# Two of four layer norms: results written by ScalarE with a scale and a shift instead of by VectorE

## The chip, the core and the metric

The kernel runs on one NeuronCore of a Trainium2 chip. The core has a matrix engine (TensorE, "PE" in the profile, with its weight loads as "PEld"), VectorE ("DVE"), ScalarE ("ACT"), GpSimd ("POOL") and SyncE ("SP", which here only issues transfers). Each engine works through its own queue of instructions in order. Where an instruction needs another engine's result it waits for a semaphore, and everything behind it in its queue waits too.

The metric is the device time of one execution in microseconds, smaller is better. The time before is 2995.68 us, the median of 3 runs (2994.83 to 2996.52).

## The reference

Two graph layers are applied one after the other to 64 graphs of 256 nodes with 256 features, in float32. The first is a pair of graph attention steps, a layer norm, a feed-forward block with relu and a second layer norm. The second is an attention of 8 heads whose values depend on the relation between two nodes, a third layer norm, a feed-forward block with gelu and a fourth layer norm. Cut to what matters here:

```python
def _layernorm(x, g, b):
    mu = jnp.mean(x, axis=-1, keepdims=True)
    var = jnp.var(x, axis=-1, keepdims=True)
    return (x - mu) * jax.lax.rsqrt(var + EPS) * g + b

# layer 0
h = _gat(_gat(x, adj, W1, a1, F), adj, W2, a2, F)
h = _layernorm(x + h, g_ln1, b_ln1)                        # first norm, "A"
ff = relu(h @ w_ff1 + b_ff1) @ w_ff2 + b_ff2
src = _layernorm(h + ff, g_ln2, b_ln2)                     # second norm, "B"
# layer 1
attn_out = heads(src, adj) @ Wo + bo
x = _ln(src + attn_out, g1, beta1)                         # third norm, "C"
ff = gelu(x @ W1 + b1) @ W2 + b2
out = _ln(x + ff, g2, beta2)                               # fourth norm, "D"
```

## The kernel before

**Tiles.** A graph's 256 nodes lie as two halves of 128 partitions with 256 features each, so a tile of node rows is 128 x 2 x 256. Matmul results land in PSUM, in eight banks that all products share in turn (`mm_tile`). Everything else is in SBUF.

**Order.** No scheduler is at work. The computation of a graph is cut into some 150 pieces with names such as `G.nmA`, and a list written out by hand (`PERIOD`, line 45) says in which order the pieces of several graphs follow each other. `F.u1/2` means: piece `F.u1` of the graph that entered two periods ago. The lags go up to 6, so parts of seven graphs are in flight. `START` fills this pipeline and `END` drains it, each with an order of its own, and the loop between them runs 58 times. Each engine gets its instructions in this order and keeps to it. Two stretches of the list matter here, with the norm pieces among the pieces around them:

```python
T.lnC/4 T.fk3/5 A.dt10/3 A.ex02/3 T.fp3/5 T.rsC/4 F.fa/2 G.gA0/1 A.mg11/3 F.u0/2 T.nmC/4 F.u1/2 T.dtC/4 ...
... T.hk2/5 G.rsA/2 T.hp1/5 A.sp01/4 A.dm01/4 T.hc/5 A.mg10/4 T.hk3/5 G.nmA/2 F.raB/4 F.dtA/2 T.hd/5 A.vk2/4 G.most/1 T.hp3/5 G.eA/1 T.hp2/5 ... T.he/5
```

**A layer norm** (`layernorm`, line 562) has three pieces. `ln` (`sums`, line 569) adds the residual and takes mean and variance on VectorE (lines 576 and 577), and ScalarE adds the small constant to the variance (line 579). `rs` (`root`, line 581) raises that to the power -1/2 on GpSimd (line 583). `nm` (`norm`, line 596) writes the result `y`: without `scalar`, by two VectorE instructions of 128 x 256 that subtract the mean and multiply by the root (line 601). With `scalar=True`, `root` has two more GpSimd instructions on 128 x 2 elements that form the shift, minus mean times root, in place of the mean (lines 586 and 587), and `norm` writes `y` by two ScalarE activations with that shift as bias and the root as scale (`norm_to`, line 591). Before the change, norm B passes `scalar=True`; norm D writes its result into PSUM in the same way (`weighted`). For A and C the input of the norm lies in PSUM (`gat_b` and `wo` in the profile), for B and D in SBUF.

**What follows a norm.** `dt` turns 32 x 32 squares of `y` on VectorE (line 542, `sq_a`, `sq_c`), `dm` and `mg` store them to device memory and load them back rearranged (lines 546 and 553, issued by SP), so that features lie on partitions (`cols_a`, `cols_c`). `ra` and `rb` multiply `y` by the gain and add the shift of the norm on GpSimd (lines 629 and 634), for the next residual.

**Products.** The two products of a feed-forward block and the projections are done by seven products of quarter size instead of eight (`seven_products`, line 692). Their pieces are `ha` to `he` for the first product and `fa` to `fe` for the second, in PSUM banks X, Y and Z. Banks X and Y keep on accumulating while results are taken out in between: `hk1`, `hk2`, `hk3`, `hk4` are copies out of a bank by ScalarE (line 770, tile `hid_c` or `hid_a`), `hp1`, `hp2`, `hp3` are adds by VectorE (line 734). So `T.he` may begin only once `T.hp2` has read bank X (`hX_c`). The second product needs sums of quarters of the hidden tile, made by GpSimd in `F.u0` to `F.u3` (line 676, tile `H_a`): `F.fb` needs `u0`, `F.fc` needs `u1` and then `u3`, `F.fd` needs `u2`.

Of the kernel before, what the change touches and what calls it, by code (L numbers as in the profile page):

```python
# [210 lines left out]
def binary(ctx: ExitStack, tc: tile.TileContext, t, most, out: bass.AP):  # L211

    nc = tc.nc
    x, xT, adjT = t["x"], t["xT"], t["adjT"]
# [18 lines left out]
    def mm_tile(name, shape=(P, 2, 256)):  # L233
        return psum.tile(list(shape), F32, tag="mm", name=name, bufs=8)
# [195 lines left out]
    graphs, tiles, warmed = {0: {}}, {}, []  # L430
# [98 lines left out]
    def over_nodes(name):  # L529
        return rows[name].unsqueeze(1).to_broadcast([P, NT, D])  # L530
# [31 lines left out]
    def layernorm(do, stage, key, name, src, last=None, scalar=False):  # L562

        tiles = {}

        def sums():
            acc, *residual = src()
            if residual:  # L570
                nc.vector.tensor_tensor(acc, acc, *residual, ALU.add)
            tiles["acc"] = acc
            stats = small.tile([P, NT, 6], F32, tag="stats", name=f"stats_{name}", bufs=2)
            mv = tiles["mv"] = small.tile([P, NT, 2], F32, tag="mv", name=f"mv_{name}")
            for i in range(NT):
                nc.vector.bn_stats(stats[:, i, :], acc[:, i, :])
                nc.vector.bn_aggr(mv[:, i, :], stats[:, i, :])
            tiles["var"] = small.tile([P, NT], F32, tag="var", name=f"var_{name}")
            nc.scalar.activation(tiles["var"], mv[:, :, 1], AF.Identity, bias=eps)

        def root():
            tiles["rstd"] = small.tile([P, NT], F32, tag="rstd", name=f"rstd_{name}")
            nc.gpsimd.tensor_tensor(tiles["rstd"], tiles["var"], neghalf, ALU.pow)
            if scalar:
                tiles["shift"] = tiles["mv"][:, :, 0]
                nc.gpsimd.tensor_tensor(tiles["shift"], tiles["shift"], tiles["rstd"], ALU.mult)
                nc.gpsimd.tensor_scalar(tiles["shift"], tiles["shift"], -1.0, 1.0, ALU.mult, ALU.mult)

        def norm_to(y):
            for i in range(NT):  # L590
                nc.scalar.activation(
                    y[:, i, :], tiles["acc"][:, i, :], AF.Identity,
                    bias=tiles["shift"][:, i : i + 1], scale=tiles["rstd"][:, i : i + 1],
                )

        def norm():
            y = tiles["y"] = work.tile([P, NT, D], F32, tag="y", name=f"y_{name}", bufs=3)
            if scalar:
                return norm_to(y)
            for i in range(NT):  # L600
                nc.vector.tensor_scalar(
                    y[:, i, :], tiles["acc"][:, i, :],
                    tiles["mv"][:, i, 0:1], tiles["rstd"][:, i : i + 1], ALU.subtract, ALU.mult,
                )

        def weighted():

            tiles["n"] = mm_tile(f"n_{name}")
            norm_to(tiles["n"])

        def finished():
            tiles["res"] = work.tile([P, NT, D], F32, tag="res", name=f"res_{name}", bufs=3)
            nc.vector.tensor_tensor(tiles["n"], tiles["n"], over_nodes(last[0]), ALU.mult)
            nc.vector.tensor_tensor(tiles["res"], tiles["n"], over_nodes(last[1]), ALU.add)

        do[f"{stage}.ln{key}"], do[f"{stage}.rs{key}"] = sums, root
        if last:
            do[f"{stage}.nm{key}"], do[f"{stage}.rb{key}"] = weighted, finished
        else:
            do[f"{stage}.nm{key}"] = norm  # L620
        return tiles

    def scaled(do, stage, key, name, tiles, g, b):


        def times():
            tiles["res"] = work.tile([P, NT, D], F32, tag="res", name=f"res_{name}", bufs=3)
            for i in range(NT):
                nc.gpsimd.tensor_tensor(
                    tiles["res"][:, i, :], tiles["y"][:, i, :], rows[g], ALU.mult  # L630
                )

        def plus():
            nc.gpsimd.tensor_tensor(tiles["res"], tiles["res"], over_nodes(b), ALU.add)

        do[f"{stage}.ra{key}"], do[f"{stage}.rb{key}"] = times, plus

    def to_columns(do, stage, key, name, tiles, pairs=False):

        def out():
            sq = work.tile([P, 4, NT * KC * 32], F32, tag="sq", name=f"sq_{name}", bufs=2)
            flat = sq.rearrange("p b n -> p (b n)")
            if pairs:
                return flat, sq.rearrange("p b (t r k) -> p t k b r", t=NT, k=KC)
            return flat, flat

        def rows():
            y = tiles["y"]  # L650
            if pairs:
                return y.rearrange("p t (k b c) -> p t k b c", k=KC, b=4)
            return y.rearrange("p t (k b c) -> p b (t k) c", k=KC, b=4)

        def into():
            cols = work.tile([P, KC * N], F32, tag="cols", name=f"cols_{name}", bufs=3)
            if pairs:
                tiles["cols"] = cols.rearrange("p (n k) -> p k n", k=KC)
            else:
                tiles["cols"] = cols.rearrange("p (a t k r) -> p k t a r", a=4, t=NT, k=KC)  # L660
            return cols.rearrange("p (a n) -> p a n", a=4)

        turned(do, stage, key, f"y_{name}", P, rows, into, out)
# [14 lines left out]
    def combine(do, stage, key, name, tiles):  # L678


        def sums():
            s = tiles["S"] = work.tile([P, 4, P], F32, tag="S", name=f"S_{name}", bufs=3)
            cols = tiles["cols"]
            blocks = [block(cols, c, i) for i in range(NT) for c in range(KC)]
            sums = [s[:, n, :] for n in range(4)]
            if len(blocks[0].shape) == 3:
                sums = [n.rearrange("p (a r) -> p a r", a=4) for n in sums]
            add_sums(nc.gpsimd, blocks, sums, range(4))

        do[f"{stage}.s{key}"] = sums  # L690
# [133 lines left out]
    def gat(do, b, tiles):  # L824


        t = {}
# [123 lines left out]
            do[f"G.ad{step}"], do[f"G.ex{step}"] = partial(maximum, step), partial(exps, step)  # L951
            do[f"G.rz{step}"] = partial(over_sums, step, width)
        do["G.gB"] = second
        return layernorm(do, "G", "A", f"a{b}", lambda: (t["gat"], tiles["x"]))

    def projections(do, b, tiles):

# [168 lines left out]
    def graph(b, do, tiles):  # L1126
        a = gat(do, b, tiles)
        to_columns(do, "F", "A", f"a{b}", a)
        scaled(do, "F", "A", f"a{b}", a, "L0_gnn_g_ln1", "L0_gnn_b_ln1")
        combine(do, "F", "A", f"a{b}", a)  # L1130
        feed_forward(do, "F", f"a{b}", a, lambda: ff0, "r", AF.Relu)
        y = layernorm(do, "F", "B", f"b{b}", lambda: (a["ff"],), scalar=True)
        to_columns(do, "F", "B", f"y{b}", y, pairs=True)
        scaled(do, "F", "B", f"b{b}", y, "L0_gnn_g_ln2", "L0_gnn_b_ln2")
        combine(do, "F", "B", f"y{b}", y)
        heads = attention(do, b, projections(do, b, y), tiles)
        c = layernorm(do, "T", "C", f"c{b}", lambda: (heads["wo"], y["res"]))
        to_columns(do, "T", "C", f"c{b}", c)
        scaled(do, "T", "C", f"c{b}", c, "L1_gnn_g1", "L1_gnn_beta1")
        combine(do, "T", "C", f"c{b}", c)  # L1140
        feed_forward(do, "T", f"c{b}", c, ff1, "ge", AF.Gelu, b >= B - LAST)
        d = layernorm(
            do, "T", "D", f"d{b}", lambda: (c["ff"],), ("L1_gnn_g2", "L1_gnn_beta2"), True
        )

        def store():
            nc.sync.dma_start(out=out[b].rearrange("(t p) d -> p t d", p=P), in_=d["res"])

        do["T.out"] = store


    E = mybir.EngineType
    graph(0, graphs[0], tiles[0])
    order = [(piece, int(lag)) for piece, lag in (entry.split("/") for entry in PERIOD)]
    lags = max(lag for _, lag in order)

    def run(piece, b):
        if piece.startswith("S."):
            return setup.pop(piece)()
        if piece.startswith("W."):  # L1160
            return warm(4, wx[:, 0, :D])
        if b not in graphs:
            graphs[b] = {}
            graph(b, graphs[b], load(graphs[b], b))
        graphs[b].pop(piece)()

    with tc.manual_schedule(engines={E.PE, E.DVE, E.Activation, E.Pool, E.SP}):
        for entry in START:
            piece, b = entry.split(":")
# [4 lines left out]
        for entry in END:  # L1174
            piece, b = entry.split(":")
# [306 lines left out]
```

## Time and profile before

| | |
|---|---|
| median of 3 runs | 2995.68 us |
| the profiled execution | 2995.85 us |
| its span, from the first to the last instruction | 2994.0 us |
| ScalarE: `y_b` (line 591), mean of one | 593 ns, 128 times |
| VectorE: `y_a` and `y_c` (line 601), mean of one | 540 and 531 ns, 128 times each |
| GpSimd: `rstd_a`, `rstd_c` (line 583), mean of one | 702 and 701 ns, 64 times each |
| GpSimd: `mv_b` lines 586 and 587, mean of one | 197 and 193 ns, 64 times each |
| GpSimd: `mv_d` lines 586 and 587, mean of one | 208 and 490 ns, 64 times each |
| mean granted TensorE clock | 0.995 of full speed |

The span is a little shorter than the execution's time, because that also holds what lies before the first and after the last instruction of the program. Busy times count an engine's own work and not its waiting. Instructions of one engine overlap at their ends, so the distance between two starts can be shorter than the duration shown. A row such as `y_a<-gat_b,mv_a,rstd_a` names the tile written and the tiles read. In a timeline, `x2` are two like instructions shown as one row, and a bracket tells how long the engine sat idle before the row and whose instruction ended that.

### The profile page before, as it was taken

The page shows a single profiled execution, that of the slowest core. Times are in us where ns is not written, and L with a number is a line of the kernel's source. Part 1 is how long each engine was busy: PE and PEld are TensorE (multiplying, and loading weights), DVE is VectorE, ACT ScalarE, POOL GpSimd, SP SyncE. Part 2 cuts the span into 40 slices and gives each one's busy share as a digit, 9 for nine tenths or more (in the row PEclk, how much of TensorE's full clock was granted, in tenths as well). Part 3 has the DMA queues.
Part 4 walks back from the last instruction along what each step waited for, and adds up shares of the span by engine and source line. Part 5 has one row for each costly group of instructions (what it writes and reads, how often), then busy time and mean ns, then how long its engine had stood idle before and what let it go on. Part 6 is the DMA issues. An engine that isn't in the chain of part 4 may idle for free.

```text
span 2994.0 us, 75422 instructions
## 1 busy us (share of the span) xinstructions
PE 2947.4 (98%) x25662; PEld 2673.7 (89%) x25662; DVE 2603.0 (87%) x6250; ACT 2234.8 (75%) x6401; POOL 2287.4 (76%) x3455
## 2 busy tenths in 40 slices
PE   8999999999999999999999999999999999999997
PEld 7889999999999999999899999999899998999986
DVE  4888889888889888898898898888898898898885
ACT  3677787787777777777777777777777877877764
POOL 6777778777777777778778778777777787777785
PEclk9999999999999999999999999999999999999999
DMA  5544444444444444444454444454444444444442
GB/s 138 157 149 158 151 148 157 153 148 159 149 150 156 147 152 153 151 153 154 151 155 152 153 156 149 152 159 146 149 160 149 152 157 152 146 159 151 132 156 86
DMA packets 401891, 449.27 MB, mean 150 GB/s; under 512 B 41152, under 2 KB 342720, under 8 KB 401504
## 3 DMA queue, kind: packets, MB, share of 16 engines
q1 hardware_dynamic: 399984, 442.14, 46.3%
q8 instruction: 209, 3.42, 0.5%
q0 software_dynamic: 976, 1.72, 0.3%
q14 instruction: 178, 1.46, 0.2%
q10 hardware_dynamic: 544, 0.52, 0.1%
HBM read 242.90 MB, written 201.33 MB: 148 GB/s over the span
## 4 chain that ended last, share of the span: by engine, by line
PE 91%; POOL 3%; DVE 2%; DMA 2%; issue 1%; ACT 1%; SPq 0%; POOLq 0%; DVEq 0%; ACTq 0%
PE hX_a L758 8%; PE o L1082 8%; PE fX_a L796 7%; PE hX_c L758 7%; PE fX_c L796 7%; PE sc L1024 4%; PE wo L1103 4%; PE qX L967 4%; PE hY_a L758 4%; PE hY_c L758 4%; PE fY_c L796 4%; PE fY_a L796 4%; PE gat_a L930 3%; PE wh L847 3%; PE gat_b L930 3%; PE vX L991 3%
## 5 line engine op out<-in xcount | busy, mean ns | idle before, releaser
L1071 DVE SCALAR_TENSOR_TENSOR pm<-away,pm 128x512 f32<-128x512 uint8 x512 | 359.2, 712 | 4.6 <-DMA pm<-far_p 4.2
L542 DVE STREAM_TRANSPOSE p<-p 128x1024 f32<-128x1024 f32 x256 | 315.4, 1232 | 4.2 <-POOL p L1057 4.1
L1082 PE MATMUL o<-pm,v 128*32 128x256 f32 x4096 | 235.4, 381 | 0.1
L776 ACT ACTIVATE hid_c<-hid_c,col_L_gnn_b 128x256 f32<-128x256 f32 x512 | 231.5, 505 | 1.7 <-DVE hid_c L734 0.4
L776 ACT ACTIVATE hid_a<-hid_a,col_L_gnn_b_ff 128x256 f32<-128x256 f32 x512 | 224.4, 501 | 2.2 <-DVE hid_a L734 2.0
L796 PE MATMUL fX_a<-f_L_gnn_w_ff,hid_a 128*128 128x128 f32 x1536 | 203.8, 276 | 1.7 <-DVE acc_a L734 1.3
L796 PEld LDWEIGHTS fX_a<-f_L_gnn_w_ff,hid_a 128*128 128x128 f32 x1536 | 196.0, 192 | 10.5 <-DVE acc_a L734 2.3
L796 PE MATMUL fX_c<-f_L_gnn_W,hid_c 128*128 128x128 f32 x1536 | 203.5, 275 | 0.8 <-DVE acc_c L734 0.4
L1082 PEld LDWEIGHTS o<-pm,v 128*32 128x32 f32 x4096 | 126.5, 110 | 85.5 <-issue 0.9
L796 PEld LDWEIGHTS fX_c<-f_L_gnn_W,hid_c 128*128 128x128 f32 x1536 | 191.8, 192 | 5.6 <-DVE acc_c L734 0.6
L770 ACT COPY hid_a<-hX_a 128x512 f32<-128x512 f32 x192 | 113.2, 590 | 60.5 <-PE hX_a L758 60.1
L676 POOL TENSOR_TENSOR S_y<-cols_y 128x128 f32<-128x128 f32 x128 | 65.5, 512 | 118.7 <-DMA cols_y<-far_y_y 118.4
L1024 PE MATMUL sc<-kT,qT 32*128 32x256 f32 x2048 | 146.6, 400 | 2.5 <-DVE kT L988 2.4
L758 PE MATMUL hX_a<-S_a,f_L_gnn_w_ff 128*128 128x128 f32 x1024 | 144.1, 284 | 0.0
L864 ACT COPY wh_B<-gat_a 128x258 f32<-128x258 f32 x124 | 46.4, 375 | 129.7 <-PE gat_a L930 129.7
L758 PEld LDWEIGHTS hX_c<-cols_c,f_L_gnn_W 128*128 128x128 f32 x1024 | 131.1, 191 | 13.0 <-DVE hid_c L734 3.1
L758 PEld LDWEIGHTS hX_a<-S_a,f_L_gnn_w_ff 128*128 128x128 f32 x1024 | 124.0, 191 | 19.6 <-issue 19.2
L758 PE MATMUL hY_c<-S_c,f_L_gnn_W 128*128 128x128 f32 x1024 | 139.5, 279 | 0.0
L796 PE MATMUL fY_a<-f_L_gnn_w_ff,H_a 128*128 128x128 f32 x1024 | 137.8, 277 | 0.7 <-DVE acc_a L809 0.6
L758 PE MATMUL hX_c<-cols_c,f_L_gnn_W 128*128 128x128 f32 x1024 | 135.3, 275 | 2.8 <-DVE hid_c L734 2.5
L796 PE MATMUL fY_c<-f_L_gnn_W,H_c 128*128 128x128 f32 x1024 | 136.4, 276 | 1.5 <-POOL H_c L676 0.9
L758 PE MATMUL hX_a<-cols_a,f_L_gnn_w_ff 128*128 128x128 f32 x1024 | 135.9, 276 | 0.0
(2845 smaller groups left out, 10573.6 us busy)
## 6 DMA issues: line engine op xcount, KB each, us to landing
far_p<-p SPq DMA_DIRECT2D x256, 512.0 KB, 3.0
pm<-far_p SPq DMA_DIRECT2D x1024, 128.0 KB, 2.9
adj<-in_adjT SPq DMA_DIRECT2D x64, 256.0 KB, 3.3
far_y_a<-sq_a SPq DMA_DIRECT2D x64, 256.0 KB, 2.1
cols_a<-far_y_a SPq DMA_DIRECT2D x256, 64.0 KB, 2.0
far_y_y<-sq_y SPq DMA_DIRECT2D x64, 256.0 KB, 2.0
cols_y<-far_y_y SPq DMA_DIRECT2D x256, 64.0 KB, 2.0
far_y_c<-sq_c SPq DMA_DIRECT2D x64, 256.0 KB, 2.0
```

What stands on the lines that cost most here:

```text
L542: nc.vector.transpose(to, rows)
L758: nc.tensor.matmul(ps[:, f * P : (f + 1) * P], weights()[0][:, factor, f * P : (f + 1) * P], left, start=start and f == 0, stop=f == FC // ...
L770: nc.scalar.copy(hidden(i, h), ps.rearrange("p (f n) -> p f n", n=P))
L776: nc.scalar.activation(tiles["hid"][:, f, :], tiles["hid"][:, f, :], func, bias=b1[:, f : f + 1])
L796: nc.tensor.matmul(ps, left[:, f, :], weights()[2][:, factor, f * P : (f + 1) * P], start=start and f == 0, stop=f == FC // 2 - 1, skip_gr ...
L847: nc.tensor.matmul(t["whp", j], tiles["xT"][:, c, nodes(j)], wx[:, c, :], start=(c == 0), stop=(c == KC - 1),)
L930: nc.tensor.matmul(ps, t["s"][:, j, nodes(i)], t["whz"][:, j, :width], start=(j == 0), stop=(j == NT - 1),)
L967: nc.tensor.matmul(ps[:, nodes(n)], w[:, factor, :], right, start=start and n == 0, stop=n == 1, skip_group_check=True,)
L1024: nc.tensor.matmul(t["sc", g, hh][:, i, :], qkv["q"][hd, g, nodes(i)], qkv["k"][hd, g, :], start=True, stop=True,)
L1071: nc.vector.scalar_tensor_tensor(pm[:, 1], tiles["away"].rearrange("p (a n) -> p a n", a=4), 0.0, pm[:, 0], ALU.is_equal, ALU.mult,)
L1082: nc.tensor.matmul(ps[hh * DH : (hh + 1) * DH, :], qkv["v"][:, j, d0 : d0 + DH], t["pm", (g, hh)][:, r].rearrange("p a (j t r) -> p j t a ...
L1103: nc.tensor.matmul(t["wo"][:, i, :], t["oT"][:, c, nodes(i)], late["wo"][:, c, :], start=(c == 0), stop=(c == KC - 1),)
```

## The change

Norms A and C now pass `scalar=True` as norm B does. Nothing else is touched: `PERIOD`, `START` and `END` stay as they are, and the pieces `G.rsA`, `G.nmA`, `T.rsC` and `T.nmC` keep their places in them.

```diff
-        return layernorm(do, "G", "A", f"a{b}", lambda: (t["gat"], tiles["x"]))
+        return layernorm(do, "G", "A", f"a{b}", lambda: (t["gat"], tiles["x"]), scalar=True)
...
-        c = layernorm(do, "T", "C", f"c{b}", lambda: (heads["wo"], y["res"]))
+        c = layernorm(do, "T", "C", f"c{b}", lambda: (heads["wo"], y["res"]), scalar=True)
```

For each graph VectorE loses four instructions (two of line 601 for each norm), ScalarE gains four of line 591, and GpSimd gains two of line 586 and two of line 587. On ScalarE the new instructions of A stand between the copy of `T.hk3` (`hid_c<-hX_c`) and `G.most` (`adj`, line 839), and those of C between the exponentials of `A.ex02` and `A.ex03`. On GpSimd they stand right behind `rstd_a` and `rstd_c`; behind those of C come `F.u0`, `F.u1`, `F.u3` and `F.u2`. TensorE's and SP's instructions and their order are the same.

## The prediction

> **What bounds the kernel now.** I read first the busy times of the page and the chain of waits:
>
> ```profile
> PE 2947.4 (98%) x25662; PEld 2673.7 (89%) x25662; DVE 2603.0 (87%) x6250; ACT 2234.8 (75%) x6401; POOL 2287.4 (76%) x3455
> ...
> PE 91%; POOL 3%; DVE 2%; DMA 2%; issue 1%; ACT 1%; SPq 0%; POOLq 0%; DVEq 0%; ACTq 0%
> ```
>
> TensorE is busy in all but 46.6 us of the span (2994.0 - 2947.4), and 91% of the chain is its own work. So unloading VectorE saves almost nothing; what counts is whether anything that TensorE waits for comes later. In the longest pieces of the chain the wo product (L1103) starts at 1893.41 and again at 1938.54: a period is 45.13 us. The written order runs 58 such periods (lag 6 of 64 graphs), each with one first norm (A) and one third norm (C).
>
> So I read one period, engine by engine, in the timeline (start, duration, engine, line; in brackets idle time and who ended it). First norm, VectorE, ScalarE and the weight loads:
>
> ```profile
> 1596.74 0.99 DVE L601 TENSOR_SCALAR y_a<-gat_b,mv_a,rstd_a 128x256 f32<-128x256 f32 x2
> 1597.77 0.71 DVE L542 STREAM_TRANSPOSE sq_a<-y_a 128x512 f32<-128x512 f32 x1
> 1598.41 0.38 DVE L1006 TENSOR_TENSOR v<-vY,row_bv 128x256 f32<-128x256 f32 x1
> 1598.71 0.67 DVE L734 TENSOR_TENSOR hid_c<-hid_c,hY_c 128x512 f32<-128x512 f32 x1
> 1599.48 0.69 DVE L734 TENSOR_TENSOR hid_c<-hid_c,hX_c 128x512 f32<-128x512 f32 x1
> ```
> ```profile
> 1597.58 0.59 ACT L770 COPY hid_c<-hX_c 128x512 f32<-128x512 f32 x1 [0.31 <-PE hX_c L758]
> 1598.06 0.73 ACT L839 ACTIVATE adj<-adj,minus_one 128x512 int32<-128x512 int32 x1
> ```
> ```profile
> 1586.22 0.97 PEld L796 LDWEIGHTS fY_a<-f_L_gnn_w_ff,H_a 128*128 128x128 f32 x8
> ...
> 1600.22 0.89 PEld L758 LDWEIGHTS hX_c<-cols_c,f_L_gnn_W 128*128 128x128 f32 x7
> ```
>
> The last product into hX_c (T.he) starts loading weights at 1600.22, and the add that must first read hX_c out of its bank (T.hp2) ends at 1599.48 + 0.69 = 1600.17. That is 0.05 us, and it is 51 to 53 ns for the same two instructions in 60 of the 64 graphs: **this add has no slack at all** before TensorE. It stands fourth on VectorE behind y_a.
>
> Third norm, GpSimd:
>
> ```profile
> 1581.53 0.70 POOL L583 TENSOR_TENSOR rstd_c<-var_c,neghalf 128x2 f32<-128x2 f32 x1 [1.12 <-ACT var_c L579]
> 1582.19 1.28 POOL L676 TENSOR_TENSOR H_a<-hid_a 128x512 f32<-128x512 f32 x1
> 1583.55 1.27 POOL L676 TENSOR_TENSOR H_a<-H_a,hid_a 128x512 f32<-128x512 f32 x1
> 1584.90 1.27 POOL L676 TENSOR_TENSOR H_a<-hid_a,H_a 128x512 f32<-128x512 f32 x1
> ```
>
> The third H_a (F.u3) ends at 1586.17 and the weight load of fY_a that takes it starts at 1586.22, again 0.05 us, in 61 graphs of 64. Three adds queue right behind rstd_c, which itself waited for var_c, so for TensorE's wo product through VectorE: the chain hangs on TensorE and can't start earlier.
>
> **What the change costs, part by part.** Removed: two TENSOR_SCALAR on VectorE for each norm, 0.99 us a pair for A, 0.98 for C (L601). Added for each norm: two small GpSimd operations (L586, L587) behind rstd, and a pair of ScalarE activations (L591). The second norm shows the prices:
>
> ```profile
> 1592.73 0.84 POOL L583 TENSOR_TENSOR rstd_b<-var_b,neghalf 128x2 f32<-128x2 f32 x1 [0.88 <-ACT var_b L579]
> 1593.65 0.20 POOL L586 TENSOR_TENSOR mv_b<-mv_b,rstd_b 128x2 f32<-128x2 f32 x1
> 1593.94 0.19 POOL L587 TENSOR_SCALAR mv_b<-mv_b 128x2 f32<-128x2 f32 x1
> ```
>
> *GpSimd.* From the end of rstd_b (1593.57) to the end of L587 (1594.13): 0.56 us. The fourth norm's row gives the upper end: rstd_d ends at 1611.61, its L587 at 1612.50, 0.89 us, because L587 took 0.52 there while VectorE ran a masking multiply (pm, L1071). Beside the new operations of A and C VectorE stands waiting for y, so I take 0.56.
>
> The Trainium skill ("SBUF — State Buffer", "Who interferes with whom") says that a VectorE operation with two SBUF inputs shuts GpSimd out of a port that they share until it ends. The 0.52 beside pm agrees; by the rule the price is 0.56 where no such operation runs, and 0.89 where one does, some 19 us more over 58 periods.
>
> *ScalarE.* The nearest row is y_b, 1.09 us the pair, but from SBUF; y_a and y_c are read from PSUM. Pairs with a bias column take 0.91 from SBUF (hid_a, L776) and 0.84 from PSUM (s_B, L884), so I take 1.09 - 0.08 = 1.01. Ends: 0.84 (that s_B, without a scale column) and 1.20 (n_d, written to PSUM).
>
> *First norm, on the path.* The activations stand behind the copy of hX_c, which waits for TensorE, so they start at 1598.06, where adj starts now; mv_a is ready by 1596.71 + 0.56 = 1597.27. y_a is done at 1599.07 instead of 1597.73. VectorE has nothing it may do meanwhile: its queue is in order, and sq_a is next. Then sq_a at 1599.10, v at 1599.74 (+0.64, as now), the two hid_c adds at 1600.04 (+0.30) and 1600.64 (+0.60, the usual step of such an add), the last ending at 1601.33: 1.16 us later than 1600.17. The weight loader idles 0.10 before 1600.22 now, so I count half of that off: **1.11 us a period** (0.89 to 1.35 with the ends of the pair, and all or none of the 0.10). What else comes late finds TensorE late too: the gelus of hid_c behind y_a wait for the same add; ScalarE's qT and kT copies move about 1.2 us, and so do the products around them. On SP the store of sq_a moves from 1598.51 to about 1599.85 and holds up the loads of cols_y behind it. cols_y lands at 1602.32 and is used from 1603.45 on: both move by about the same, and the 1.1 us between them remain. Were that cover gone, it would cost up to 0.2 us a period.
>
> *Third norm, on the path.* H_a comes 0.56 later at each of its steps. The first had 0.6 us of slack (weight load at 1584.07, add over at 1583.47), the second 0.46, the third none: **0.56 us a period** (0.46 to 0.89). ScalarE waits 0.5 us for mv_c with the exponentials queued behind it, and y_c is done at 1582.83 + 1.01 = 1583.84, 0.32 later than now. I cost both at nothing: ScalarE idles 1.21 us before its next copy (wh_B at 1584.48) and reaches it some 0.2 late, just before e_B; VectorE idles 0.54 before 1585.37. Without these covers they would run beside the 0.56 and not on top of it.
>
> *Fill and drain.* In the first 173 and last 149 us TensorE is busy 155.9 and 121.9 us. Six norms of each kind lie there. If all hit TensorE as above they cost 6 x 1.67 = 10 us; if VectorE's queue ends each wait they save 12 x 0.98 = 12. I take nothing.
>
> Sum: 58 x (1.11 + 0.56) = 97 us. The profiled execution took 2995.85 us (span 2994.0), 0.17 above the median of the runs, so 2995.7 + 97 = **3092 us**.
>
> Two sentences of the Trainium skill pull against each other here. "ScalarE: Activation LUTs" ("Rules for kernel authors") wants additions and products on VectorE, and "Perfetto Trace Analysis" ("Optimizing Scalar/DVE Operations") lets work go from VectorE to ScalarE once VectorE is saturated. VectorE's 87% would invite the second, at best for the 46.6 us that TensorE idles, 2949 us; the two gaps of 0.05 us say that neither decides, since queue places set the price.
>
> **Rivals.** (1) *Only one of the two stalls lands*, the other meeting slack that one period doesn't show: 58 x 1.11 gives 3060, 58 x 0.56 gives 3028. Against: the 0.05 us repeats in 60 and in 61 graphs. (2) *More queues suffer*: ScalarE carries 2.0 us more work a period, and products of q and k (0.5 us between ScalarE's copy ending at 1604.74 and the product at 1605.24) or the landing of cols_y stall too. With 0.5 us a period more, 29 us: 3121. For: the order leaves little air. Against: all of these sit behind the stall and move with TensorE. (3) *Faster*: VectorE's queue gets its 0.99 us back ahead of T.hp2, because y_a is written before sq_a's turn. It decides if y_a ends on ScalarE before 1597.73; then TensorE loses only part of its 46.6 us of idling, say 30: 2966. Against: y_a would have to start at 1596.7, ahead of a copy that stands before it and waits for TensorE until 1597.58. (4) *The operations don't move*: the built order of both kernels shows y_a on ScalarE right behind the hX_c copy and y_c between two pairs of exponentials, so this gets 1%, at 2996.
>
> **Chances.** Forecast 0.68, rival 1 0.12, rival 2 0.14, rival 3 0.03, no change 0.03 (rival 4, or everything hidden). A measurement tells some 0.2%, 6 us, from no change. Corner sums are 58 x (0.89 + 0.46) - 12 = 66 and 58 x (1.35 + 0.89) + 10 = 140 us; with part of rivals 1 and 2 the range is 3058 to 3130. Faster 0.03, same 0.03, slower 0.94.
>
> **What would show it.** A period of about 46.8 us; VectorE idle some 1.4 us before sq_a, released by ScalarE's y_a; TensorE idle before T.he about 1.1 us, released by VectorE's hid_c, and about 0.5 before fY_a, released by GpSimd's H_a; both new waits in every period. Wrong if the period stays below 45.6 us, if the idle time of TensorE sits at other products, or if y_a starts on ScalarE before 1598.06 of this period's time.

## The result, and the profile after

The changed kernel takes 3098.07 us (median of 4 runs, 3096.15 to 3098.76), the kernel before beside it 2996.10 us (2994.83 to 2997.69). The ratio is **1.0342, with a 95% interval of 1.0329 to 1.0354: 3.4% slower**. The prediction was 3092 us, range 3058 to 3130.

The busy times of the page of the changed kernel:

```profile
PE 3003.0 (97%) x25662; PEld 2674.9 (86%) x25662; DVE 2473.2 (80%) x5994; ACT 2348.3 (76%) x6657; POOL 2341.9 (76%) x3711
```

VectorE is 130 us less busy than before (2603.0) and ScalarE 114 us more (2234.8), so the change did what it says. TensorE has the same 25662 products and 56 us more of modelled busy time, which is a warning: its ends are modelled, and the weight loads, whose busy time stays at 2674.9 us (2673.7 before), don't show it, so I take it for waiting that is counted as work. The weight loads show the waits better. What the weight loads and VectorE waited for, in total, how often, and the longest, in the changed kernel:

```profile
PEld hX_c L758 <- DVE hid_c L734: 54.8, 60, 1.9
PEld vY L991 <- DVE v L1006: 29.4, 58, 0.5
...
PEld fY_a L796 <- POOL H_a L676: 23.3, 61, 0.7
```
```profile
DVE sq_a L542 <- ACT y_a L591: 152.2, 63, 3.1
DVE sq_c L542 <- ACT y_c L591: 78.1, 62, 1.9
```

In the kernel before, the weight loads of hX_c waited for hid_c 3.1 us in all, three times, and those of fY_a for H_a 0.6 us, twice. Here they come about once a period. VectorE's new idle time (230 us) is far more than the total loss: most of it costs nothing, and only what delays TensorE counts.

One period, first norm, in the timeline of the changed kernel: ScalarE, VectorE, weight loads.

```profile
1604.55 0.59 ACT L770 COPY hid_c<-hX_c 128x512 f32<-128x512 f32 x1 [0.31 <-PE hX_c L758]
1605.03 1.03 ACT L591 ACTIVATE y_a<-gat_b,mv_a,rstd_a 128x256 f32<-128x256 f32 x2
```
```profile
1602.98 0.65 DVE L734 TENSOR_TENSOR hid_c<-hid_c,hZ_c 128x512 f32<-128x512 f32 x1
1606.09 0.71 DVE L542 STREAM_TRANSPOSE sq_a<-y_a 128x512 f32<-128x512 f32 x1 [2.46 <-ACT y_a L591]
1606.72 0.39 DVE L1006 TENSOR_TENSOR v<-vY,row_bv 128x256 f32<-128x256 f32 x1
1607.03 0.67 DVE L734 TENSOR_TENSOR hid_c<-hid_c,hY_c 128x512 f32<-128x512 f32 x1
1607.63 0.67 DVE L734 TENSOR_TENSOR hid_c<-hid_c,hX_c 128x512 f32<-128x512 f32 x1
```
```profile
1607.16 0.30 PEld L991 LDWEIGHTS vY<-f_Wv,S_y 128*128 128x128 f32 x2 [0.51 <-DVE v L1006]
1608.35 0.97 PEld L758 LDWEIGHTS hX_c<-cols_c,f_L_gnn_W 128*128 128x128 f32 x8 [0.89 <-DVE hid_c L734]
```

y_a starts 0.48 us after the start of the copy, where adj stood before, and VectorE stands idle for 2.46 us with sq_a at the head of its queue. The last add of hX_c ends at 1608.30 and the weight load follows at 1608.35, the same 0.05 us as before. The weight loads show two pauses, 0.51 and 0.89 us; the first is an earlier station of the same delay.

Third norm, GpSimd and the weight load that takes its third sum:

```profile
1587.94 0.70 POOL L583 TENSOR_TENSOR rstd_c<-var_c,neghalf 128x2 f32<-128x2 f32 x1 [1.33 <-ACT var_c L579]
1588.72 0.20 POOL L586 TENSOR_TENSOR mv_c<-mv_c,rstd_c 128x2 f32<-128x2 f32 x1
1589.01 0.19 POOL L587 TENSOR_SCALAR mv_c<-mv_c 128x2 f32<-128x2 f32 x1
1589.17 1.27 POOL L676 TENSOR_TENSOR H_a<-hid_a 128x512 f32<-128x512 f32 x1
1590.51 1.28 POOL L676 TENSOR_TENSOR H_a<-H_a,hid_a 128x512 f32<-128x512 f32 x1
1591.87 1.27 POOL L676 TENSOR_TENSOR H_a<-hid_a,H_a 128x512 f32<-128x512 f32 x1
```
```profile
1593.19 0.97 PEld L796 LDWEIGHTS fY_a<-f_L_gnn_w_ff,H_a 128*128 128x128 f32 x8 [0.38 <-POOL H_a L676]
```

The small operations end 0.56 us after rstd_c (1589.20 - 1588.64). The three sums follow, and the last ends 0.05 us before the weight load again.

**Where the 103 us of the profiled executions went** (spans 3097.0 and 2994.0). I compared the distances between the starts of neighbouring weight loads in the two traces, step by step in the periodic part. Only a few steps grew:

| Step | a period, median |
|---|---|
| the loads for vY and the last product into hX_c, 0.482 - 0.107 + 0.797 - 0.036 | +1.14 us |
| the loads that take the second and the third sum H_a, 0.141 + 0.413 | +0.55 us |
| the period, from one wo product to the next | 45.13 to 46.82, +1.69 us |

On average over the periods it is 1.63 us and not 1.69: in the kernel before, the loads of cols_y land late now and then, and 0.09 us a period of that now hides behind the new wait. From the second wo product to the sixtieth, 58 periods, the time grew from 2624.8 to 2719.1 us, by 94.3. The part before that grew by 2.8 us and the part after it by 5.9.

### The profile page after: what moved, and what is told of

Same layout as the page of the kernel before. It is cut to its first block, busy times and chain, and to the rows that moved or that the text cites. A ratio compares the mean times of both kernels' runs of the same rounds, so it can differ in the third digit from the quotient of the medians.

```text
span 3097.0 us, 75750 instructions
## 1 busy us (share of the span) xinstructions
PE 3003.0 (97%) x25662; PEld 2674.9 (86%) x25662; DVE 2473.2 (80%) x5994; ACT 2348.3 (76%) x6657; POOL 2341.9 (76%) x3711
## 5 line engine op out<-in xcount | busy, mean ns | idle before, releaser
L1071 DVE SCALAR_TENSOR_TENSOR pm<-away,pm 128x512 f32<-128x512 uint8 x512 | 348.9, 693 | 5.0 <-DMA pm<-far_p 4.6
L676 POOL TENSOR_TENSOR S_y<-cols_y 128x128 f32<-128x128 f32 x128 | 76.3, 596 | 139.2 <-DMA cols_y<-far_y_y 139.2
L542 DVE STREAM_TRANSPOSE sq_a<-y_a 128x512 f32<-128x512 f32 x64 | 45.6, 712 | 152.2 <-ACT y_a L591 152.2
L796 PEld LDWEIGHTS fY_a<-f_L_gnn_w_ff,H_a 128*128 128x128 f32 x1024 | 128.6, 191 | 27.7 <-POOL H_a L676 23.3
```

The lines of the kernel that those rows point to most:

```text
L542: nc.vector.transpose(to, rows)
L676: engine.tensor_tensor(to[i], one, other, op)
L796: nc.tensor.matmul(ps, left[:, f, :], weights()[2][:, factor, f * P : (f + 1) * P], start=start and f == 0, stop=f == FC // 2 - 1, skip_gr ...
L1071: nc.vector.scalar_tensor_tensor(pm[:, 1], tiles["away"].rearrange("p (a n) -> p a n", a=4), 0.0, pm[:, 0], ALU.is_equal, ALU.mult,)
```

## The experiments

Each run is compared with the kernel before on the same chip; the period is the median distance of the wo products. The medians of the kernel before lie between 2992.22 and 2996.10 us on the chips used, so a difference between two absolute times is good to some 4 us.

| Run | median, us | ratio to before, 95% interval | period, us |
|---|---|---|---|
| the change | 3098.07 | 1.0342 (1.0329 to 1.0354) | 46.82 |
| first norm alone | 3055.51 | 1.0201 (1.0184 to 1.0218) | 46.26 |
| third norm alone | 3030.20 | 1.0113 (1.0096 to 1.0130) | 45.68 |
| small GpSimd steps alone | 3025.66 | 1.0098 (1.0081 to 1.0115) | 45.68 |
| first sum ahead of the root | 3149.25 | 1.0508 (1.0490 to 1.0525) | 47.75 |
| turning later | 3074.15 | 1.0272 (1.0255 to 1.0289) | 46.31 |
| turning later, loads first | 3065.96 | 1.0245 (1.0228 to 1.0262) | 46.21 |
| y_a ahead of the copy | 3069.00 | 1.0254 (1.0237 to 1.0271) | 46.24 |
| all three moves | 3118.55 | 1.0418 (1.0401 to 1.0436) | 47.17 |
| shifts on VectorE | 3099.86 | 1.0351 (1.0334 to 1.0368) | 46.87 |
| third norm, shift on VectorE | 3037.21 | 1.0140 (1.0124 to 1.0157) | 45.74 |
| shifts on VectorE, y_a ahead | 3063.48 | 1.0231 (1.0214 to 1.0248) | 46.18 |
| third norm, shift on ScalarE | 3000.63 | 1.0024 (1.0014 to 1.0033) | 45.13 |

### One norm at a time

```diff
-        c = layernorm(do, "T", "C", f"c{b}", lambda: (heads["wo"], y["res"]), scalar=True)
+        c = layernorm(do, "T", "C", f"c{b}", lambda: (heads["wo"], y["res"]))
```

> Only the first norm is written by ScalarE; the third stays on VectorE. Theory (two separate stalls, each set by a place in a queue, which add): TensorE waits some 1.14 us a period before the last product into hX_c, and no longer before fY_a; 58 periods give 66 us, and about half of the 9 us of fill and drain comes on top: 3065 to 3070 us. Rival (the loss is the extra work of ScalarE, which is the same for both norms): half of the 102 us, 3047 us.

It took 3055.51 us. The wait is the one of the full change to the last digit, and there is none before fY_a:

```profile
PEld hX_c L758 <- DVE hid_c L734: 54.8, 60, 1.9
PEld vY L991 <- DVE v L1006: 29.4, 58, 0.5
```

The period grew by 1.13 us, 1.14 expected. The total is 10 us below my figure, because the periods grew by 60.2 us and not 66 (the landings of cols_y that now hide), and fill and drain lost nothing.

The other way round, with the first norm's call put back and the third's left as changed:

> Only the third norm is written by ScalarE; the first stays on VectorE. Theory: 0.55 us a period before fY_a, released by GpSimd's H_a, nothing before the last product into hX_c; 32 us and some 4 us of fill and drain: 3030 to 3035 us. Rival (extra work of ScalarE): 3047 us. Rival (the third norm's stall is there only because the first norm's stall has moved TensorE): 2996 to 3002 us.

3030.20 us, as the first theory had it. The weight loads of this run have one new wait:

```profile
PEld fY_a L796 <- POOL H_a L676: 23.2, 61, 0.7
```

The same amount, as often, as in the full change (23.3 us, 61 times): the stall doesn't need the first norm's. Period growths of 1.13 and 0.55 add up to the 1.69 of both, within 0.01. An even share of ScalarE's extra work (3047 us for either run) is refuted.

### The third norm: which of its parts costs the time

The kernel before, with the two operations added and nothing moved:

```diff
+            if stage == "T" and not scalar:
+                spare = tiles["var"]
+                nc.gpsimd.tensor_tensor(spare, tiles["mv"][:, :, 0], tiles["rstd"], ALU.mult)
+                nc.gpsimd.tensor_scalar(spare, spare, -1.0, 1.0, ALU.mult, ALU.mult)
```

> The kernel before, with the two small GpSimd operations of the shift added behind rstd_c for the third norm, into a tile that nothing reads; VectorE still writes y_c. Theory (the third norm's loss is the GpSimd queue alone): as with the third norm on ScalarE, 0.55 us a period before fY_a, 3028 to 3033 us. Rival (the loss comes from VectorE and ScalarE waiting for y_c): no change, 2996 us.

3025.66 us, and a period of 45.68 us, the same as with the third norm on ScalarE:

```profile
PEld fY_a L800 <- POOL H_a L680: 23.4, 61, 0.7
```

Two operations on 256 numbers each, whose result nobody reads, cost 30 us, because three sums that TensorE waits for stand behind them.

Then I tried to take them out of the way by order:

```diff
-A.ex02/3 T.fp3/5 T.rsC/4 F.fa/2 G.gA0/1 A.mg11/3 F.u0/2 T.nmC/4 F.u1/2 T.dtC/4 F.fk1/2 A.rz02/3
+A.ex02/3 T.fp3/5 F.u0/2 T.rsC/4 F.fa/2 G.gA0/1 A.mg11/3 T.nmC/4 F.u1/2 T.dtC/4 F.fk1/2 A.rz02/3
```

> Both norms on ScalarE; in the periodic order alone, the first sum for the feed-forward block (F.u0) stands before the third norm's root on GpSimd. Theory: the first sum then runs while GpSimd waits for the variance, the three sums end about 0.6 us earlier, and the wait before fY_a goes: a period of 46.3 us, 3098 - 32 = 3066 us. Rival (the wait is not of this queue): 3098 us.

The theory's number was wrong by 83 us: 3149.25, slower than the change itself. GpSimd in one period of this run, the weight load, and what the products behind it waited for in the whole run:

```profile
1566.12 1.27 POOL L676 TENSOR_TENSOR H_a<-hid_a 128x512 f32<-128x512 f32 x1 [1.68 <-PE fY_c L796]
1567.35 0.70 POOL L583 TENSOR_TENSOR rstd_c<-var_c,neghalf 128x2 f32<-128x2 f32 x1
```
```profile
1569.78 0.97 PEld L796 LDWEIGHTS fY_a<-f_L_gnn_w_ff,H_a 128*128 128x128 f32 x8 [1.49 <-issue]
```
```profile
PE fY_a L796 <- ACT y_c L591: 64.2, 58, 1.4
```

I had overlooked two dependencies. The first sum can't start early: `H_a` and `H_c` share one buffer (`bufs=1`), so it waits for the product fY_c to have read the old one, and now the root waits behind it. And fY_a's bank in PSUM is the one that y_c is read from (the wo bank, handed on when y_c is done). With the root late, y_c was late, and TensorE lost 1.35 us before fY_a; the profile names ScalarE's y_c for 58 waits of the product fY_a, 64.2 us. What this run does show is that a later y_c is a second price of the third norm. In this run y_c ends 0.11 us ahead of the first weight load of fY_a (median); in the full change it ends 0.23 us ahead, 0.55 in the kernel before, and the step before that load is 0.22 us in both, so there the second price isn't paid.

### The first norm: places in the queues

Both norms on ScalarE, the turning of y_a two adds later in VectorE's queue:

```diff
-T.hk3/5 G.nmA/2 F.raB/4 F.dtA/2 T.hd/5 A.vk2/4 G.most/1 T.hp3/5 G.eA/1 T.hp2/5 T.ge0/5 F.dmB/3
+T.hk3/5 G.nmA/2 F.raB/4 T.hd/5 A.vk2/4 G.most/1 T.hp3/5 F.dtA/2 G.eA/1 T.hp2/5 T.ge0/5 F.dmB/3
```

> Both norms on ScalarE; in the periodic order alone, the turning of y_a on VectorE (F.dtA) stands two adds later, just ahead of T.hp2. Theory (the first norm's loss is VectorE standing idle at the turning with the adds of hX_c behind it): the two pieces before it fill the wait, T.hp2 ends some 0.36 us later than in the kernel before in place of 1.16, so 0.7 to 0.8 us a period come back, less up to 0.15 where the loads of cols_y wait on SP behind the store of sq_a: 3050 to 3064 us. Rival (ScalarE's added work delays what follows on ScalarE): 3098 us.

3074.15 us: 24 us come back (21 by the ratios), less than the 34 to 48 expected. The wait before the last product into hX_c fell from 1.14 to 0.34 us a period, as worked out. But TensorE now waits elsewhere (products of this run):

```profile
PE qX L967 <- DMA cols_y<-far_y_y: 11.6, 15, 1.8
```

The step before qX grew by 0.28 us in the median and 0.37 on average. TensorE arrives there 0.8 us earlier than in the changed kernel, while the loads of cols_y still wait on SP behind the late store of sq_a. The 1.1 us that I called cover were read in one period. In the median the last load of cols_y lands 0.56 us ahead of the first weight load of qX in the kernel before, 0.78 in the changed one, where the stall holds TensorE back too, and 0.10 here. So the next run puts the loads first (`F.mgB` ahead of `F.dmA`):

> As the run with the turning two adds later, and on SP the loads of cols_y stand before the store of sq_a. Theory: if the loads of cols_y were late there, up to 0.15 us a period comes back, 3045 to 3055 us; if the 1.1 us between their landing and their use cover it, the same time as without. If the store of sq_a now comes so late that cols_a is not there in time, slower than without.

3065.96 us. The wait for cols_y is gone, and 0.14 us a period appear at the next accumulation into qX instead. ScalarE's copy kT, which has to be done before it, ends 0.11 us ahead of that weight load, against 0.30 in the kernel before. The trace names no releaser there, so that it is ScalarE's added work in `y_a` is likely and not shown.

The other handle is ScalarE's queue:

```diff
-T.hk3/5 G.nmA/2 F.raB/4 F.dtA/2 T.hd/5 ...
+G.nmA/2 T.hk3/5 F.raB/4 F.dtA/2 T.hd/5 ...
```

> Both norms on ScalarE; in the periodic order alone, y_a stands on ScalarE ahead of the copy of hX_c (T.hk3) and not behind it. Theory (places in queues): y_a starts when the shift is ready, some 0.75 us earlier; the copy behind it ends 0.6 us later, and TensorE waits 0.6 us for that copy, and at the last product into hX_c no more than that: 0.6 in place of 1.14 us a period, 3098 - 31 = 3067 us. Rival (the amount of work on ScalarE): 3098 us.

3069.00 us against 3067 expected. The wait moved to the product that needs the copy, 0.57 us a period, and nothing is left before the last product:

```profile
PE hX_c L758 <- ACT hid_c L770: 17.4, 58, 0.6
```

Every engine does the same work as in the changed kernel and 29 us are gone (26 by the ratios): the price is set by who stands behind whom. GpSimd's two small operations have no part in the first norm's price: in the run of the next section that makes both shifts on VectorE, the loads for vY and the last product into hX_c lose 1.13 us a period, against 1.14 in the change.

The three moves that were to help, together:

> Both norms on ScalarE with the three moves in the periodic order together: first sum before the root, turning two adds later, loads of cols_y before the store of sq_a. Theory: what is left are about 0.35 us a period before the last product into hX_c and 9 us of fill and drain: 3020 to 3030 us, not below the kernel before, since VectorE's lighter queue gives TensorE nothing. Rival (VectorE's 2 us less a period are worth something once the stalls are gone): below 2996 us.

3118.55 us. It carries the failed first sum with it (the same 1.35 us a period before fY_a) and the half-cured first norm, so it says nothing on VectorE's relief.

### The shift made elsewhere

Both norms on ScalarE, the shift by one VectorE instruction of 128 x 2 ahead of the activations:

```diff
-                nc.gpsimd.tensor_tensor(tiles["shift"], tiles["shift"], tiles["rstd"], ALU.mult)
-                nc.gpsimd.tensor_scalar(tiles["shift"], tiles["shift"], -1.0, 1.0, ALU.mult, ALU.mult)
...
+                    nc.vector.scalar_tensor_tensor(
+                        tiles["shift"], tiles["shift"], -1.0, tiles["rstd"], ALU.mult, ALU.mult
+                    )
```

> Both norms on ScalarE, the shift (minus mean times root) of both by one small VectorE instruction ahead of the activations, in place of two on GpSimd; the sums for the feed-forward block keep their place behind the root. Theory (the third norm's loss is the time of the two small operations in GpSimd's queue): the wait before fY_a goes, the one before the last product into hX_c stays at 1.14 us a period, a period of 46.27 us, 3062 to 3070 us. Rival (y_c written by ScalarE costs the time in another way, through the PSUM bank that fY_a takes over from it): 3098 us.

> The third norm alone on ScalarE, its shift by VectorE; the first norm on VectorE as before. VectorE has some 0.8 us less a period and ScalarE 1.0 us more. Theory: no wait is new in the periods (45.13 us); the drain keeps up to 6 us: 2996 to 3004 us, not faster than before. Rival (VectorE's lighter queue is worth something once nothing is late): below 2990 us.

> Both norms on ScalarE, both shifts by VectorE, and y_a ahead of the copy of hX_c on ScalarE. Theory (the two losses add and each is cut by its own edit): 0.45 to 0.57 us a period before the third product into hX_c, which waits for the copy, and nothing else: 3028 to 3040 us. Rival (with one wait gone the other takes its time back): 3062 us or more.

All three missed: 3099.86, 3037.21 and 3063.48 us. VectorE, ScalarE and GpSimd in the run with the third norm alone:

```profile
1647.44 0.93 DVE L601 SCALAR_TENSOR_TENSOR mv_c<-mv_c,rstd_c 128x2 f32<-128x2 f32 x1
1649.47 0.71 DVE L542 STREAM_TRANSPOSE sq_c<-y_c 128x512 f32<-128x512 f32 x1 [1.09 <-ACT y_c L592]
```
```profile
1648.41 1.02 ACT L592 ACTIVATE y_c<-wo,mv_c,rstd_c 128x256 f32<-128x256 f32 x2 [1.15 <-DVE mv_c L601]
```
```profile
1647.10 1.26 POOL L681 TENSOR_TENSOR H_a<-hid_a 128x512 f32<-128x512 f32 x1
```

The instruction on 256 numbers took 0.93 us. It began while GpSimd added `H_a` and ended with it (1648.37 and 1648.36). A reciprocal of the same 128 x 2 elements, with one input, took 0.14 us some 3 us later, beside GpSimd's third sum. So y_c came 0.7 us later than with the shift on GpSimd (6.44 in place of 5.75 us from the first wo load to the start of y_c, median), and the second price fell due: in this run the product fY_a waits for ScalarE's y_c,

```profile
PE fY_a L801 <- ACT y_c L592: 13.6, 58, 0.2
```

and the steps around it grew by 0.60 us a period: 0.47 at the first loads of fY_a, and 0.17 at the load of e_B, which follows 0.05 us behind the copy wh_B that stands behind y_c on ScalarE, less 0.05 at the third sum. The run with both norms and y_a ahead of the copy has the same 0.60 us and, as expected, 0.45 before the product that needs the copy, so its 3063.48 us lie in its rival's range for another reason. The sums were in time and the time was lost all the same, so these runs can't decide whether the GpSimd steps were the only cause in the change. The last run leaves those steps out without making y_c late. The third norm alone, with the mean negated by VectorE right behind the statistics, and the product by ScalarE:

```diff
+            if scalar and key in "AC":
+                nc.vector.tensor_scalar(mv[:, :, 0], mv[:, :, 0], -1.0, 1.0, ALU.mult, ALU.mult)
...
+                    for i in range(NT):
+                        nc.scalar.activation(
+                            tiles["shift"][:, i : i + 1], tiles["shift"][:, i : i + 1], AF.Copy,
+                            scale=tiles["rstd"][:, i : i + 1],
+                        )
```

> The third norm alone on ScalarE, the first on VectorE as before. The shift is made without GpSimd: VectorE negates the mean right behind the statistics, and ScalarE multiplies it by the root in two instructions of 128 x 1 just ahead of y_c. Nothing is added behind rstd_c in GpSimd's queue, and y_c ends when it does with the two GpSimd operations. Theory (the third norm's 0.55 us a period are GpSimd's two operations ahead of the three sums): at most 0.1 us a period is left, where the copy behind y_c reaches e_B late; with up to 6 us of drain 2996 to 3008 us. Rival (y_c's later end, which frees the PSUM bank that fY_a takes over, is enough by itself): 3025 us or more. Rival (VectorE's lighter queue is worth something): below 2990 us.

3000.63 us, and a period of 45.13 us, that of the kernel before. Its weight loads hardly wait for H_a:

```profile
PEld fY_a L805 <- POOL H_a L685: 0.6, 2, 0.4
```

So y_c on ScalarE is free in the periods once nothing is added ahead of the sums and y_c isn't late. The expectation had it that y_c ends as late as in the change. It ended 0.13 us later than in the kernel before (median) and not 0.32, so this run alone doesn't refute the rival of the later y_c; that is done by the run with the small steps alone, which loses the same 0.55 us with y_c where it was, and by the unchanged step before the first load of fY_a in the change. And VectorE's relief is worth nothing there: it is busy for 2556.5 us in place of 2603.0, and the 58 periods take 2624.1 us in place of 2624.8. The 0.24% that remain lie in fill and drain. No version that I tried is faster than the kernel before.

## Why the prediction was right

- *What bounds the kernel.* TensorE, with two releases that leave 0.05 us. Right: the same two instructions release TensorE at the same 0.05 us, about once a period.
- *First norm, 1.11 us a period.* Measured 1.14, and 1.13 by itself. Place and size of its parts held: y_a at the place of adj, 1.03 us for the pair (1.01 taken), sq_a at the head of VectorE's queue. The first station, the load for vY waiting 0.5 us for v, wasn't named; it lies within the same delay.
- *Third norm, 0.56 us a period.* Measured 0.55, by the two GpSimd operations alone. The choice of 0.56 against 0.89 held, beside VectorE's last add into acc_c and then an idle VectorE. Costing y_c's own lateness at nothing was right for this kernel, with too little reason given: the PSUM bank that passes from wo to fY_a wasn't in the account, and with y_c 0.7 us later it decides. The copy wh_B, which was in the account, now ends 0.05 us ahead of e_B's load (0.21 before), so that cover was just used up.
- *Fill and drain, nothing.* Measured 2.8 + 5.9 = 8.7 us. This is the mis-sized term, inside the bounds of -12 and +10 that were given. The 5.9 go with the third norm: in one profiled execution each, the part from the sixtieth wo product on took 196.0 us before, 192.5 with the first norm alone and 202.4 with the third alone. Which wait makes it wasn't read. The last 149 us that the prediction looked at leave some 59 periods ahead of them; behind 58 periods stand 196 us.
- *The sum.* 58 x 1.67 = 97 against 94.3, since part of the late landings of cols_y hides behind the new wait; together with fill and drain 103.0 against 97. The two misses, 2.7 us too much in the periods and 8.7 too little outside, partly cancel.
- *Signs.* VectorE's idle time before sq_a was given as 1.4 us a period and is 2.4 (152.2 us over 63 waits), since the 0.99 us of y_a that leave VectorE's queue weren't added to it. The sum doesn't use it. The period (46.82 us), the two waits and their releasers came as given, with a part of the first wait at the load for vY.
- *Rivals.* One stall only: refuted by each norm alone. More queues suffering: not in the changed kernel, but the slack was as small as feared: moving the turning met the next wait (cols_y, then the accumulation into qX). The 1.1 us of cover for cols_y were those of one period; 0.56 us, to the weight load, is the median. Faster: refuted; with y_a ahead of the copy the copy is late instead, and VectorE's relief gave TensorE nothing. Instructions that don't move: refuted by the counts.

## What to carry to other kernels

Here one engine is busy nearly all the time and the orders are fixed. Moving work off a busy second engine gained nothing, and its price could be read from two things: which release has no slack, and what stands ahead of it in the same queue. Count small helper operations by the place they take: 0.56 us of arithmetic on 256 numbers, ahead of three sums that were just in time, was a third of this loss. Before a piece is moved earlier, look up whose buffer and whose PSUM bank it takes over, since neither shows in the dataflow.

## What the runs showed of the hardware

- A VectorE instruction with two small SBUF inputs (128 x 2) took 0.93 us beside a GpSimd add that ran over it, and ended with it. The Trainium skill ("SBUF — State Buffer", "Who interferes with whom") says that a VectorE instruction with two SBUF inputs contends with a GpSimd instruction that reads SBUF, and that the port pair they share is an exclusive lock; the prediction used it for GpSimd waiting on VectorE, and this run shows the other direction. But the same instruction of the first norm, in the run with both shifts on VectorE, took 0.16 us inside a GpSimd scaling of `p` by a column that had begun 0.05 us before it (59 graphs of 64):

```profile
1416.48 0.16 DVE L601 SCALAR_TENSOR_TENSOR mv_a<-mv_a,rstd_a 128x2 f32<-128x2 f32 x1
1416.43 0.93 POOL L1062 TENSOR_SCALAR p<-p,arz_(0, 1)_17765 128x256 f32<-128x256 f32 x2
```

  So running beside a GpSimd instruction that reads SBUF isn't enough to make it long. What sets the two cases apart is not shown.
- The same activation with a scale and a shift column took 594 ns on average from SBUF (y_b) and 568 and 561 ns from PSUM (y_a, y_c).
